# Recurrent layer: ScalarE copies the gate's projection out of its bank, and VectorE multiplies it from memory

## The chip, the cores and the metric

The kernel runs on one core of a Trainium2 chip. A core has five engines with a queue of instructions each: TensorE (PE in the profile, with PEld for its weight loads), VectorE (DVE), ScalarE (ACT), GpSimd (POOL) and SyncE (SP, which issues DMAs here). Each engine works through its queue in order, and semaphores hold an instruction back until what it needs is done. TensorE writes its results into banks of an accumulation memory (PSUM); the other tiles lie in on-chip memory (SBUF). The metric is the device time of one execution in microseconds (us).

## The reference

Four layers run one after the other on x (32 x 64 x 256) with a context of the same shape: a cross-attention of channels (L0), two decoder layers with self-attention, cross-attention and an MLP (L1, L2), and a recurrent layer (L3). Only L3 matters here. Cut to that, it is:

```python
xn  = _ln(x, ln1_w, ln1_b)
sx  = _token_shift(xn, state[:, i1])
xxx = tanh((xn + sx * maa_x) @ maa_w1)          # five mixes of 32 each
xxx = matmul(xxx.reshape(b, l, 5, 1, 32), maa_w2).reshape(b, l, 5, E)
x5  = xn[:, :, None] + sx[:, :, None] * (maa_stack + xxx)
w   = exp(-exp(time_decay + tanh(x5[:, :, 1] @ decay_w1) @ decay_w2))
r, k, v = x5[:, :, 3] @ Wr.T, x5[:, :, 0] @ Wk.T, x5[:, :, 2] @ Wv.T
g   = silu(x5[:, :, 4] @ Wg.T)                  # the gate
# along the sequence, for each head, with a_t = k_t (outer) v_t:
#   out_t = r_t . (u * a_t + s);   s = a_t + w_t * s
att = groupnorm(outs) * gn_w + gn_b
x   = x + att * g @ Wo.T
xn2 = _ln(x, ln2_w, ln2_b);  sx2 = _token_shift(xn2, state[:, i0])
rr  = sigmoid((xn2 + sx2 * ffn_maa_r) @ ffn_Wr.T)
kk  = square(relu((xn2 + sx2 * ffn_maa_k) @ ffn_Wk.T))
return x + rr * (kk @ ffn_Wv.T)
```

## The kernel before

The 2048 tokens are held in four groups; the recurrent layer takes them in eight chunks of 256 tokens (four sequences of 64), numbered n = 0 to 7. A chunk's tiles are [128, 2, 256] in fp32: 128 of the 256 channels on the partitions, the two halves of the channels, and the tokens. In the profile a tile's name ends in `_r` for all chunks alike (`gt_r`, `pg_r`).

The function `recurrent` returns three lists of steps for a chunk. The first holds `norm`, `first_mix`, `maa`, `mix(2, 3)`, `vals`, `mix(0, 1)`, `recept`, `keys`, `mix(4)`, `decay_a`, `decay_b`, `own_term` and `gate`. Four of them use `project`, which multiplies a mix by a weight into a bank: `vals` (bank `pv`), `recept` (`pr`), `keys` (`pk`) and `gate` (`pg`). ScalarE copies `pr` to `rT` (L729); VectorE multiplies `pk` by `rT` into `rk` (L736), which the matmul of `own_term` reads into `pcf` (L742). The mixes are evacuated by VectorE (L689), then GpSimd adds the normed x (L692).

The gate works with a tanh, since silu(p) is half of p * (tanh(p / 2) + 1); the half lies in the weights of the group norm. ScalarE makes the tanh from the bank (L772), and VectorE adds 1 and multiplies by the projection, read from the bank a second time (L773). The result `gt` is needed much later, when `norm_b` multiplies the attention by it (L834).

The second list holds the recurrence: DMAs spread the values over the heads into `vb` (L725), VectorE multiplies them by the keys (L782 in `outer`), ScalarE writes four columns of the state s0 into them (L787), VectorE runs four scans along the tokens (L797) and multiplies by the recept `rT` (L782 again, in `read`), and TensorE sums over the keys into `pa` (L132). This is done for e = 0 and 1. Then come the group norm (L815 to L834) and the output projection `pwo` (L843). The third list is the feed-forward part with `pkk`, `pfr` and `pfv`.

Banks are taken from rings: the tag `mm` has two, `sc` two, `tp` two, `pc` and `pd` one each. `project` takes `mm` for `vals`, `recept`, `keys` and `gate`; the MLP halves of layer L2 (`pln_L2m` for their norm, `pf_L2m` for their hidden layer), which run interleaved with the first chunks, take `mm` too. Whoever takes a bank waits for the last reader of the tile that had it before. Tiles in SBUF are taken from rings in the same way: `gt` has two buffers, `rk` one.

All steps get a due time in units of a chunk's slot, are sorted by it (`timed`, `emit`), and a scheduler that estimates times then sets the order on every engine.

Of the kernel before, what the change touches and what calls it, by code (L numbers as in the profile page):

```python
# [18 lines left out]
ALU = mybir.AluOpType  # L19
# [61 lines left out]
def tile_xattn_stack(ctx: ExitStack, tc: tile.TileContext, a: dict, out: bass.AP):  # L81
    nc = tc.nc
# [519 lines left out]
    def recurrent(n, pool, c3):  # L602

        g, u = n // 2, n % 2
# [11 lines left out]
        def tile_(name, bufs=2, shape=None, p=pool, tag=None):  # L616
            return p.tile(shape or [P, 2, RR], FP, tag=tag or name, name=f"{name}_{t}", bufs=bufs)
# [82 lines left out]
        def project(w, x, name, tag="mm"):  # L700
            ps = both(f"p{name}_{t}", tag)
            for o in range(2):
                project_T(ps[:, o], c3[w], slice(o * P, (o + 1) * P), x)
            return ps
# [63 lines left out]
        def gate():  # L768

            gt = st["gt"] = tile_("gt")  # L770
            ps = project("Wg", st["x5", 4], "g")
            nc.scalar.activation(gt, ps, AF.Tanh, scale=0.5)  # L772
            nc.vector.scalar_tensor_tensor(gt, gt, 1.0, ps, ALU.add, ALU.mult)  # L773

        first = [(0.5, lambda: norm("x", "L3_ln1_w", "L3_ln1_b", t, 1)), (0.0, first_mix), (1.2, maa)]
        first += [(0.85, lambda: mix(2, 3)), (1.7, vals), (0.85, lambda: mix(0, 1)), (1.7, recept), (1.7, keys)]
        first += [(0.85, lambda: mix(4)), (0.5, decay_a), (0.85, decay_b), (0.85, own_term), (1.7, gate)]


# [460 lines left out]
```

## Time and profile before

| | us |
|---|---|
| runs | 1083.98, 1085.02, 1078.87 (median 1083.98) |
| the profiled execution | 1080.68 |
| its span | 1078.9 |
| recurrent layer with the last MLP halves | about 705 to 1079 |
| gates (L772 to L773), first and last start | 749.1 to 1035.3 |

An engine's busy time says how much it works, not what sets the end. For that one reads the chain that ended last, which follows each instruction back to what released it, and the waits: which engine stood still, before which instruction, and what ended it. The timeline of a short window shows the queues side by side. Its columns are the start, the time taken, the engine, the line, the operation, the tiles written and read, the shape and the number of instructions merged in the row; in brackets stands the idle time of the engine before it, and the line that ended that. Rows of several instructions are merged over others in between, so a row's time can hold gaps.

### The profile page before, as it was taken

To read this page: it belongs to the slowest core of one execution; us is meant where nothing else is said; L and a number is where in the kernel's file an instruction comes from. 1 tells how busy PE (TensorE), PEld (TensorE's weight loads), DVE (VectorE), ACT (ScalarE), POOL (GpSimd) and SP (SyncE) were. 2 spreads that over 40 slices of the span, in tenths; PEclk is the share of its full clock that TensorE was granted. 3 is DMA by queue.
4 is the path that set the end of the run, shared out by engine and by line. 5 is a ranking of instruction groups with operands and counts; after the bars stand their busy time and mean duration, and the time that the engine had idled before them with its cause. 6 is when DMAs were issued, how large, how long until landed. Compare 5 with 4: busy or idle time off the path is not lost.

```text
span 1078.9 us, 26319 instructions
## 1 busy us (share of the span) xinstructions
PE 983.6 (91%) x10764; PEld 787.8 (73%) x10764; DVE 806.2 (75%) x1513; ACT 549.2 (51%) x1271; POOL 532.2 (49%) x552
## 2 busy tenths in 40 slices
PE   8998999899989999989989999898989898988966
PEld 4886776667778989877767778787768677765645
DVE  5864688878877654777787887647887987999983
ACT  4743653554456644864454555454436464453334
POOL 4343766767657344756577665442434434153200
PEclk9999998999999999989899999999889999998889
DMA  9300111111100100140111101112122121332400
GB/s 301 105 21 21 23 45 32 38 25 27 26 22 7 40 1 21 46 138 22 41 39 28 26 21 32 31 36 66 41 70 60 50 61 40 95 76 69 98 11 29
DMA packets 45947, 53.39 MB, mean 49 GB/s; under 512 B 16146, under 2 KB 40068, under 8 KB 43780
## 3 DMA queue, kind: packets, MB, share of 16 engines
q1 hardware_dynamic: 40292, 49.60, 17.1%
q10 hardware_dynamic: 5536, 2.12, 0.8%
q8 instruction: 85, 1.39, 0.5%
q14 instruction: 34, 0.28, 0.1%
HBM read 38.83 MB, written 4.21 MB: 40 GB/s over the span
## 4 chain that ended last, share of the span: by engine, by line
PE 43%; DVE 32%; ACT 8%; POOL 8%; issue 4%; DMA 3%; SPq 0%; ACTq 0%; POOLq 0%; DVEq 0%
DVE vb_r L797 6%; PE pf_L1m L187 4%; PE pf_L2m L187 3%; DVE vb_r L782 3%; PE pfo_L1m L187 3%; POOL s_L2c L463 2%; DVE x L198 2%; POOL s_L1c L463 2%; PE pr L312 2%; PE pfo_L2m L187 2%; PE pwo_r L843 1%; PE px_r L132 1%; PE pq_L1c L187 1%; DVE s_L1c L458 1%; POOL s_L1s L463 1%
## 5 line engine op out<-in xcount | busy, mean ns | idle before, releaser
L692 POOL TENSOR_TENSOR x_r<-x_r,xn_r 128x512 f32<-128x512 f32 x40 | 63.6, 1604 | 113.7 <-DVE x_r L689 111.8
L797 DVE TENSOR_TENSOR_SCAN vb_r<-wsh,vb_r 128x512 f32<-128x512 f32 x64 | 77.6, 1276 | 5.6 <-ACT wsh L696 4.1
L463 POOL TENSOR_TENSOR s_L1s<-s_L1s,n 128x512 f32<-128x512 f32 x32 | 43.0, 1356 | 39.9 <-DVE s_L1s L458 39.2
L187 PE MATMUL pf_L2m<-lnT_L2m,w_L 128*128 128x256 f32 x384 | 57.8, 303 | 1.7 <-ACT vbd L430 0.7
L187 PEld LDWEIGHTS pf_L2m<-lnT_L2m,w_L 128*128 128x128 f32 x384 | 51.8, 202 | 7.6 <-issue 2.5
L187 PE MATMUL pfo_L2m<-w_L,hT_L2m 128*128 128x256 f32 x384 | 55.2, 291 | 1.5 <-DVE hT_L2m L581 1.5
L463 POOL TENSOR_TENSOR s_L2s<-s_L2s,n 128x512 f32<-128x512 f32 x32 | 43.0, 1360 | 26.9 <-DVE s_L2s L458 26.3
L187 PE MATMUL pfo_L1m<-w_L,hT_L1m 128*128 128x256 f32 x384 | 54.5, 288 | 1.6 <-POOL hT_L1m L580 0.8
L187 PE MATMUL pf_L1m<-lnT_L1m,w_L 128*128 128x256 f32 x384 | 51.9, 288 | 3.9 <-ACT hf_L1m L577 1.2
L463 POOL TENSOR_TENSOR s_L2c<-s_L2c,n_L2c 128x512 f32<-128x512 f32 x32 | 41.6, 1320 | 27.6 <-DVE s_L2c L458 26.7
L463 POOL TENSOR_TENSOR s_L1c<-s_L1c,n_L1c 128x512 f32<-128x512 f32 x32 | 41.3, 1309 | 25.8 <-DVE s_L1c L458 24.8
L187 PEld LDWEIGHTS pf_L1m<-lnT_L1m,w_L 128*128 128x128 f32 x384 | 47.5, 191 | 7.2 <-ACT hf_L1m L577 2.1
L187 PEld LDWEIGHTS pfo_L2m<-w_L,hT_L2m 128*128 128x128 f32 x384 | 48.7, 190 | 5.2 <-issue 2.7
L187 PEld LDWEIGHTS pfo_L1m<-w_L,hT_L1m 128*128 128x128 f32 x384 | 49.3, 191 | 3.4 <-POOL hT_L1m L580 1.0
L580 POOL TENSOR_SCALAR hT_L1m<-hf_L1m 128x512 fp32r<-128x512 f32 x32 | 21.8, 682 | 55.4 <-ACT hf_L1m L577 53.5
L577 ACT ACTIVATE hf_L1m<-pf_L1m,b_L 128x256 f32<-128x256 f32 x64 | 26.6, 471 | 42.3 <-PE pf_L1m L187 39.9
L581 DVE TENSOR_TENSOR hT_L1m<-hf_L1m,hT_L1m 128x512 fp32r<-128x512 f32 x32 | 25.3, 791 | 30.1 <-POOL hT_L1m L580 30.1
L581 DVE TENSOR_TENSOR hT_L2m<-hf_L2m,hT_L2m 128x512 fp32r<-128x512 f32 x32 | 24.7, 772 | 26.7 <-POOL hT_L2m L580 26.6
L580 POOL TENSOR_SCALAR hT_L2m<-hf_L2m 128x512 fp32r<-128x512 f32 x32 | 22.2, 694 | 40.1 <-ACT hf_L2m L577 39.8
L577 ACT ACTIVATE hf_L2m<-pf_L2m,b_L 128x256 f32<-128x256 f32 x64 | 26.6, 472 | 28.5 <-PE pf_L2m L187 23.0
L782 DVE TENSOR_TENSOR vb_r<-vb_r,ksh 128x2048 f32<-128x2048 f32 x16 | 38.3, 2409 | 2.7 <-DMA vb_r<-vd_r 2.7
L282 ACT ACTIVATE att<-pe,nmx 128x256 f32<-128x256 f32 x64 | 29.5, 476 | 19.3 <-DVE nmx L280 17.2
(388 smaller groups left out, 3062.1 us busy)
## 6 DMA issues: line engine op xcount, KB each, us to landing
vb_r<-vd_r SPq DMA_DIRECT2D x16, 1024.0 KB
raw_w_L<-in_L_w_dram SPq DMA_DIRECT2D x4, 1024.0 KB
y<-in_y_dram SPq DMA_DIRECT2D x8, 256.0 KB
x<-in_x_dram SPq DMA_DIRECT2D x8, 256.0 KB
ctxT_L1c<-in_yT_dram SPq DMA_DIRECT2D x4, 512.0 KB
kbd<-kT_L1s SPq DMA_DIRECT2D x64, 32.0 KB
kbd<-kT_L1c SPq DMA_DIRECT2D x64, 32.0 KB
kbd<-kT_L2s SPq DMA_DIRECT2D x64, 32.0 KB
```

What stands on the lines that cost most here:

```text
L132: return lambda: nc.tensor.matmul(ps, sta, mov, start=start, stop=stop)
L187: nc.tensor.matmul(ps, sta[x], mov[y], start=(at == 0), stop=(at == n - 1))
L198: nc.vector.tensor_tensor(xs, xs, ps, ALU.add)
L282: nc.scalar.activation(att[:, 2 * h + c, :], pe[:, c, :], AF.Exp, bias=nmx[:, h, c : c + 1], accum_out=rs[:, h, c : c + 1],)
L312: nc.tensor.matmul(pr[:, m, h, :], att[:, 2 * h + c, m * P : (m + 1) * P], xvT[:, c, h, :], start=(c == 0), stop=(c == 1),)
L463: nc.gpsimd.tensor_tensor(s[:, r], s[:, r], n(j).unsqueeze(1).broadcast_to([P, 8, S]), ALU.add)
L577: nc.scalar.activation(raw[:, i], ps[:, i], AF.Gelu_apprx_tanh, bias=w()["b1"][:, 2 * f2 + i : 2 * f2 + i + 1])
L580: nc.gpsimd.tensor_scalar(h[:, 0], raw, 1.0, 0.0, ALU.mult, ALU.add)
L581: nc.vector.tensor_tensor(h[:, 1], raw, h[:, 0], ALU.subtract)
L692: nc.gpsimd.tensor_tensor(d, d, st["x"], ALU.add)
L782: nc.vector.tensor_tensor(v, v, x.unsqueeze(1).broadcast_to([P, 4, 2 * RR]), ALU.mult)
L797: nc.vector.tensor_tensor_scan(v[:, d], flat(st["wsh"]), v[:, d], 0.0, ALU.mult, ALU.add)
```

## The change

In `gate`, ScalarE also copies the projection from its bank to SBUF, in the buffer of the tag `rk`, and VectorE reads the copy in place of the bank:

```diff
             gt = st["gt"] = tile_("gt")
             ps = project("Wg", st["x5", 4], "g")
             nc.scalar.activation(gt, ps, AF.Tanh, scale=0.5)
-            nc.vector.scalar_tensor_tensor(gt, gt, 1.0, ps, ALU.add, ALU.mult)
+
+            g_ = tile_("g", 1, tag="rk")
+            nc.scalar.copy(g_, ps)
+            nc.vector.scalar_tensor_tensor(gt, gt, 1.0, g_, ALU.add, ALU.mult)
```

Lines below it are three higher afterwards: the copy is L775, the multiply L776, the products by keys and recept L785, the scan L800. Nothing else is edited, but the scheduler sets the order anew. In the built program the recept projections of chunks 1 to 4 wait for a semaphore of VectorE before the change and of ScalarE after it. The order of the instructions stays the same except in the recurrent part, where a few steps move: on ScalarE and TensorE around the decay of chunk 2 (the table load and a half of the Exp of L765 and the small copies of L790 ahead of the eviction of the feed-forward norm), on TensorE `pa` of chunk 4 ahead of the mix of x5_1 of chunk 5, and in the tail ScalarE's square of chunk 7 behind the norm of chunk 6's second half.

## The prediction

> **What bounds the kernel now.** I read the page first: busy shares, then the chain that ended last.
>
> ```profile
> PE 983.6 (91%) x10764; PEld 787.8 (73%) x10764; DVE 806.2 (75%) x1513; ACT 549.2 (51%) x1271; POOL 532.2 (49%) x552
> PE 43%; DVE 32%; ACT 8%; POOL 8%; issue 4%; DMA 3%; SPq 0%; ACTq 0%; POOLq 0%; DVEq 0%
> ```
>
> No engine sets the end alone: the chain goes from TensorE (PE) to VectorE (DVE) and back. The eight gates lie between 749 and 1035 us, so what stands before 740 us stays as it is. The view of the multiply's line says who waits for it, the waits of PE between 740 and 860 us add one entry:
>
> ```profile
> L773 DVE SCALAR_TENSOR_TENSOR gt_r<-gt_r,pg_r x8: 655/674/680, 755.2 to 1035.3; 128x512 f32<-128x512 f32 x8
>   PE pr_r L192: 6.6, 2
> ```
> ```profile
> PE pr_r L192 <- DVE mv_L2m L147: 3.3, 1, 3.3
> ```
>
> So three times PE stands still before the recept projection `pr` of the next chunk: its bank is the one that held the gate's projection `pg`, and VectorE reads `pg` late because long work stands ahead in its queue. (The third wait names `mv_L2m`, the small row just behind the gate's multiply; PE starts 0.15 us after that multiply.) The timeline shows the three places, which I call gates 0, 1 and 2:
>
> ```profile
> 749.11 0.60 ACT L772 ACTIVATE gt_r<-pg_r 128x512 f32<-128x512 f32 x1 [0.66 <-PE pg_r L192]
> 751.69 1.07 PE L132 MATMUL pa_r<-vb_r,sel 128*32 128x256 f32 x16 [0.96 <-DVE vb_r L782]
> 755.21 0.66 DVE L773 SCALAR_TENSOR_TENSOR gt_r<-gt_r,pg_r 128x512 f32<-128x512 f32 x1
> 756.02 3.75 PE L192 MATMUL pr_r<-x_r,Wr 128*128 128x256 f32 x8 [3.26 <-DVE mv_L2m L147]
> ...
> 797.44 0.59 ACT L772 ACTIVATE gt_r<-pg_r 128x512 f32<-128x512 f32 x1
> 799.37 0.68 DVE L773 SCALAR_TENSOR_TENSOR gt_r<-gt_r,pg_r 128x512 f32<-128x512 f32 x1
> 799.96 2.29 DVE L782 TENSOR_TENSOR vb_r<-vb_r,rT_r 128x2048 f32<-128x2048 f32 x1
> 800.19 3.75 PE L192 MATMUL pr_r<-x_r,Wr 128*128 128x256 f32 x8 [3.21 <-DVE gt_r L773]
> ...
> 840.47 0.59 ACT L772 ACTIVATE gt_r<-pg_r 128x512 f32<-128x512 f32 x1
> 845.67 2.29 DVE L782 TENSOR_TENSOR vb_r<-vb_r,rT_r 128x2048 f32<-128x2048 f32 x1
> 845.90 2.57 PE L192 MATMUL pr_r<-x_r,Wr 128*128 128x256 f32 x8 [3.39 <-DVE gt_r L773]
> ```
>
> Stages of the stretch show what the pause does to PE's clock (columns: us, busy PE, PEld, DVE, ACT, POOL with counts, granted clock, DMA share, GB/s):
>
> ```profile
> 755.00:765.00 10.00, 8.98 (x27) 6.99 (x28) 10.00 (x20) 1.20 (x4) 5.14 (x6) 0.50 0.00 1
> 765.00:799.00 34.00, 29.43 (x215) 23.52 (x213) 28.28 (x30) 19.07 (x38) 12.00 (x9) 1.00 0.29 71
> 799.00:806.00 7.00, 5.81 (x25) 3.38 (x26) 6.33 (x12) 0.59 (x1) 1.80 (x2) 0.52 0.00 0
> ```
>
> After gates 0 and 1 the clock is half: the eight `pr` matmuls take 3.75 us, against 1.89 where the clock is full. But DVE is busy 10.00 of 10.00 and 6.33 of 7.00 us there, so what PE gains may end at DVE.
>
> **The change, part by part.** It adds eight ScalarE (ACT) copies, one per chunk. The nearest row is the same copy from a bank:
>
> ```profile
> L712 ACT COPY vT_r<-pv_r x8: 580/584/602, 721.4 to 1002.6; 128x512 f32<-128x512 f32 x8
> ```
>
> Eight times 0.58 is 4.7 us of ACT, in an engine that is 51% busy. The multiply now has both inputs in SBUF. The nearest rows with two such inputs of this size are L885 (median 690 ns against 674 for L773), so DVE neither gains nor loses: 8 times 0.016 is 0.1 us, taken as nothing. The multiply now waits for the copy, with the product by rT and the next mixes behind it in DVE's queue; DVE comes to it after the copy has ended at every gate, by 0.75 us at the tightest (gate 1: 798.6 against 799.37), so the wait adds nothing. The `rk` buffer that the copy borrows is free: `pcf`, its last reader, stands before `pg` in PE's queue, and the next `rk` product stands behind the gate's multiply in DVE's own queue. In the changed program's order `pr` waits for ACT and no longer for DVE, so the change does what it says. No DMA and no queue of SP or POOL is added or passed.
>
> *Gate 0.* The bank comes free at 749.71 + 0.58 = 750.3, PE at 752.76 (end of `pa`). So `pr` starts 3.26 us earlier, and if the clock holds it is done at 754.65 instead of 759.77. Next is the mix of x5_4, whose banks come free at DVE's L689, 756.8 either way, then the hidden layer `pf`, which waits for DVE's L179 (ends 758.17): `pf` starts at 758.3 instead of 761.7, still cold. What is late after that is `pa`, which waits for DVE's product by rT, 764.93 + 2.28 = 767.21; it ran at 770.30. So `pa` gains 3.05 us, and with it the 1 MB transfer that it releases and the product by keys that waited for that (778.72): **-3.05**.
>
> *Gate 1.* ACT ends the copy at 798.03 + 0.58 = 798.6, `pr` starts at 798.75 instead of 800.19. The next `pa` needs DVE until 802.25, and `pwo` needs DVE's second L834 (ends 804.42). `pwo` ran at 805.74; it can run at 804.5: **-1.25**.
>
> *Gate 2.* The copy ends at 841.65, so `pr` starts at 842.5 and ends at 844.4. But `pa` needs the product by rT, 845.67 + 2.29 = 847.96, and the `pf` behind it needs L179 (ends 850.91). `pf` ran at 851.75 and can run at 851.4: **-0.35**. Most of this wait is hidden behind DVE anyway. The copy puts the Ln/Exp pair and the lnT copy behind it 0.58 us later; DVE takes them 2.8 us later, which covers it.
>
> *Gates 3 to 7.* No `pr` waits for DVE there. The copies at 885.1, 967.8, 1004.4 and 1027.7 fall into idle time of ACT (0.98 to 7.6 us), cost nothing, and would cost 0.58 each if ACT were late. At gate 4 (938.73) the copy stands before the evictions L625 and L632 that free the banks of the next mix, and the new order puts `pa` (DVE is done at 940.74) ahead of both mixes. `pwo` then starts at 940.79 + 1.07 + 2.1 = 944.0, against 942.96, and DVE waits for it: **+1.0**.
>
> *Order.* The scheduler also moves steps near chunk 2's decay (820 to 833 us). ACT's table load, one half of the decay's Exp and two small copies now stand ahead of the eviction of xn_fr and sx_fr. sx_fr, done at 825.12, is done at about 827.6, so DVE idles and has three mixes (1.3 us) left in front of the scan that began at 828.01, and one behind it: by the rows 829.3 + 4.57 + 0.44 = 834.3 against 832.58: **+1.7**. In the tail, sq_r7 moves behind xn_fr's two rows (1.08 us); the table loads are the same, and Exp ends at 1057.1 instead of 1056.8: **+0.3**.
>
> Two values are unknown. The multiply may now be held up by POOL: with both inputs in SBUF, L834 ranges from 471 to 1505 ns and L885 to 1293, while rows with an input in a bank stay within 687 (L884) and 484 (L689). Bounds per gate: 0 and 0.6 us; POOL's large adds lie beside only one gate (1014.39), so I take 0 and keep +4.8 as the end. [...] The clock is the other: it is taken as it falls in the rows.
>
> Sum: -3.05 - 1.25 - 0.35 + 1.0 + 1.7 + 0.3 = **-1.65 us**. The profiled execution took 1080.68 us (span 1078.9, 1.8 around it), which gives 1079.0; it lies 3.3 below the median of the three runs, and off that median (1083.98) the sum gives **1082.3**. About 0.5%, 5.4 us, is what a measurement of this kernel can tell from no change; the three runs alone spread over 6.2.
>
> **The rivals.** *Faster: the clock.* Half clock was granted for 10.2 us after gate 0 (754.96 to 765.20), 6.8 after gate 1 and 3.4 after gate 2, 20.5 in all, which is 10.2 us of PE time lost. Without the pauses these may vanish; PE's share of the chain, 43%, makes that -4.4. If the moved steps also cost nothing, the sum is -4.65 - 4.4 = -9.05: 1075. For it: all three cold stretches follow these pauses. Against it: DVE is full there. [...]
>
> *Slower: the pause moves instead of going.* `pr` runs early, and PE then stands before `pa` and `pf`, for 2 us at gate 0 and 3.6 us at gate 2 by the sums above. The half clock then falls on hidden-layer matmuls, which are on the chain: twelve took 2.87 us cold and 1.45 warm. A cold stretch of 3.4 us on the chain costs 1.7 us. It decides from four more such stretches on: with five, -1.65 + 8.5 = +6.85: 1091. For it: the chain's PE pieces after each gate are `pf`. Against it: gate 0's were cold already.
>
> **How the numbers follow.** The forecast as summed 0.50, the clock 0.28, the moved pause 0.22. Of the forecast's 0.50, errors in six terms of 1 us, POOL's hold and the spread of runs put 0.10 below the 0.5% bound and 0.04 above it. So faster 0.28 + 0.10 = 0.38, same 0.36, slower 0.22 + 0.04 = 0.26. The forecast's own range is 1076 to 1088; with the rivals' prices it is 1074 to 1091.
>
> **What would show it.** `pr` of the next chunk should start at the end of `pa` at gate 0, and PE's waits on `gt_r` should be gone. `pa` should come 3 us earlier after gate 0, with the product by keys at 775.7. The scan of chunk 2 should start late behind DVE's mixes, `pwo` at gate 4 behind the mixes. The new copy should take 0.58 us, the multiply 0.69. Cold stretches gone from 755 to 850 would speak for the first rival; new ones on `pf` for the second. Multiplies over 1 us would make POOL the cause. If the stretch before 740 us changed, all of this would be wrong.

## The result and the profile after

The changed kernel takes 1089.51 us (median; 1086.46 to 1090.84) beside 1083.98 of the kernel before: the ratio is 1.006, with an interval of 1.0037 to 1.0083, so it is about 6.5 us slower by the ratio (the two medians lie 5.5 apart). The profiled execution is one of 1089.51 us with a span of 1087.7. Busy time and chain of the page after:

```profile
PE 988.4 (91%) x10764; PEld 789.9 (73%) x10764; DVE 803.2 (74%) x1513; ACT 553.3 (51%) x1279; POOL 532.5 (49%) x552
PE 41%; DVE 33%; POOL 9%; ACT 8%; issue 4%; DMA 2%; SPq 2%; ACTq 0%; DVEq 0%; POOLq 0%
```

PE has the same 10764 matmuls and needs 4.8 us more for them: the matmuls became slower, not more. The view of the multiply's line, and under it that of the new copy, show what the change was to do:

```profile
L776 DVE SCALAR_TENSOR_TENSOR gt_r<-gt_r,g_r x8: 658/676/684, 757.5 to 1044.3; 128x512 f32<-128x512 f32 x8
  PEld pa_r L132: 0.7, 1
...
L775 ACT COPY g_r<-pg_r x8: 574/580/647, 751.8 to 1034.5; 128x512 f32<-128x512 f32 x8
```

The 6.6 us for which `pr` had waited for this line are gone (so is the third wait, the one that named `mv_L2m`), and both prices are as forecast. The timeline of PE (and one line of DVE) shows gate 0 and gate 2:

```profile
753.85 1.07 PE L132 MATMUL pa_r<-vb_r,sel 128*32 128x256 f32 x16 [0.96 <-DVE vb_r L785]
754.85 1.99 PE L192 MATMUL pr_r<-x_r,Wr 128*128 128x256 f32 x8
760.06 3.33 PE L187 MATMUL pf_L2m<-lnT_L2m,w_L 128*128 128x256 f32 x24
769.02 2.93 PE L187 MATMUL pf_L2m<-lnT_L2m,w_L 128*128 128x256 f32 x12 [2.74 <-ACT hf_L2m L577]
...
842.74 1.89 PE L192 MATMUL pr_r<-x_r,Wr 128*128 128x256 f32 x8
845.90 2.28 DVE L785 TENSOR_TENSOR vb_r<-vb_r,rT_r 128x2048 f32<-128x2048 f32 x1
848.24 1.94 PE L132 MATMUL pa_r<-vb_r,sel 128*32 128x256 f32 x16 [3.61 <-DVE vb_r L785]
852.62 4.85 PE L187 MATMUL pf_L2m<-lnT_L2m,w_L 128*128 128x256 f32 x21
```

`pr` stands right behind the work ahead of it and is warm (at full clock; cold stands for half clock below). But `pa` waits for DVE's product by the recept, and the early bank does not bring that forward, so at gate 2 a pause of 3.61 us now lies in front of `pa`, where it was 3.39 in front of `pr`. Behind it the clock is half for 10.2 us, and the 21 hidden-layer matmuls take 4.85 us in place of 2.78, which stands in the timeline of PE before the change:

```profile
848.41 1.94 PE L132 MATMUL pa_r<-vb_r,sel 128*32 128x256 f32 x16
851.75 2.78 PE L187 MATMUL pf_L2m<-lnT_L2m,w_L 128*128 128x256 f32 x21
```

The windows of the same stretches as before, and of gate 2 (columns as before: us, the engines' busy time, granted clock, DMA share, GB/s):

```profile
755.00:765.00 10.00, 6.91 (x39) 5.59 (x40) 10.00 (x15) 2.92 (x6) 6.26 (x7) 1.00 0.00 1
799.00:806.00 7.00, 5.53 (x37) 3.54 (x36) 7.00 (x11) 2.40 (x5) 0.00 (x0) 1.00 0.00 0
...
847.00:857.50 10.50, 9.26 (x43) 6.93 (x44) 7.32 (x13) 2.07 (x3) 4.00 (x3) 0.51 0.41 100
```

The cold stretches of before are gone from the first two windows (one of 3.4 us now begins at 768.7, on the twelve hidden-layer matmuls of 2.93 us above), and a longer one has come at gate 2. Further on the timeline shows two more, at gate 4 and in the tail:

```profile
944.80 1.07 PE L132 MATMUL pa_r<-vb_r,sel 128*32 128x256 f32 x16 [2.18 <-DVE vb_r L785]
947.50 3.78 PE L846 MATMUL pwo_r<-Wo,at_r 128*128 128x256 f32 x8
953.21 3.56 PE L192 MATMUL pk_r<-x_r,Wk 128*128 128x256 f32 x8
...
1065.30 3.47 PE L846 MATMUL pwo_r<-Wo,at_r 128*128 128x256 f32 x8 [2.38 <-DVE at_r L837]
```

Eight such matmuls take 1.9 to 2.0 us at full clock. In the profile before, `pwo` at gate 4 was cold too (3.54 us) behind a pause of 1.08 us, `pk` was not, and the tail's `pwo` was warm behind a shorter pause:

```profile
939.70 1.13 PE L132 MATMUL px_r<-ta_r,mw2a 32*128 32x256 f32 x4 [1.08 <-ACT xn_r L625]
942.96 3.54 PE L843 MATMUL pwo_r<-Wo,at_r 128*128 128x256 f32 x8
947.48 1.99 PE L192 MATMUL pk_r<-x_r,Wk 128*128 128x256 f32 x8
...
1058.17 1.99 PE L843 MATMUL pwo_r<-Wo,at_r 128*128 128x256 f32 x8 [0.99 <-DVE at_r L834]
```

I followed one instruction through both traces, the large product on VectorE (L782 before, L785 after), and took the difference of its start times, counted from its first one at 736.7 us. The pieces of the profiled execution are: gate 0 -0.35, gate 1 with chunk 2's decay -1.59, gate 2 +2.41, behind it +0.34, gate 3 +1.03, gate 4 +2.88, tail +1.92. Their sum is +6.65. (The two spans differ by 8.8; the other 2.2 us lie ahead of that first product, which starts anywhere from 735.6 to 742.7 us in the sixteen profiles, with the copy and without.)

My theory from this: the pause in front of `pr` was cheap, because `pr` itself took the cold clock, and VectorE was the one that everybody waited for. Moved behind `pr`, the pause stands right in front of work on the chain, and the half clock falls on that. The rivals: the steps that the scheduler moved cost it; or ScalarE's eight copies do.

### The profile page after: what moved, and what is told of

The parts are those of the page before. It is cut to its first block, busy times and chain, and to the rows that moved or that the text cites. A ratio compares the mean times of both kernels' runs of the same rounds, so it can differ in the third digit from the quotient of the medians.

```text
span 1087.7 us, 26328 instructions
## 1 busy us (share of the span) xinstructions
PE 988.4 (91%) x10764; PEld 789.9 (73%) x10764; DVE 803.2 (74%) x1513; ACT 553.3 (51%) x1279; POOL 532.5 (49%) x552
## 4 chain that ended last, share of the span: by engine, by line
PE 41%; DVE 33%; POOL 9%; ACT 8%; issue 4%; DMA 2%; SPq 2%; ACTq 0%; DVEq 0%; POOLq 0%
DVE vb_r L800 7%; DVE vb_r L785 4%; PE pf_L1m L187 4%; PE pf_L2m L187 4%; PE pfo_L1m L187 3%; POOL s_L2c L463 2%; SPq L403 2%; POOL s_L1c L463 2%; PE pr L312 2%; DVE x L198 2%; PE pfo_L2m L187 2%; POOL s_L1s L463 1%; PE pwo_r L846 1%; PE px_r L132 1%; PE pe L132 1%
## 5 line engine op out<-in xcount | busy, mean ns | idle before, releaser
L692 POOL TENSOR_TENSOR x_r<-x_r,xn_r 128x512 f32<-128x512 f32 x40 | 66.8, 1684 | 119.0 <-DVE x_r L689 116.7
L800 DVE TENSOR_TENSOR_SCAN vb_r<-wsh,vb_r 128x512 f32<-128x512 f32 x64 | 78.4, 1286 | 4.7 <-ACT wsh L696 3.2
L187 PE MATMUL pf_L2m<-lnT_L2m,w_L 128*128 128x256 f32 x384 | 60.0, 309 | 5.4 <-ACT hf_L2m L577 3.2
L187 PE MATMUL pf_L1m<-lnT_L1m,w_L 128*128 128x256 f32 x384 | 51.9, 288 | 3.9 <-ACT hf_L1m L577 1.2
L580 POOL TENSOR_SCALAR hT_L1m<-hf_L1m 128x512 fp32r<-128x512 f32 x32 | 21.9, 685 | 55.4 <-ACT hf_L1m L577 53.5
L785 DVE TENSOR_TENSOR vb_r<-vb_r,ksh 128x2048 f32<-128x2048 f32 x16 | 38.3, 2407 | 2.9 <-DMA vb_r<-vd_r 2.9
L580 POOL TENSOR_SCALAR hT_L2m<-hf_L2m 128x512 fp32r<-128x512 f32 x32 | 21.6, 675 | 37.0 <-ACT hf_L2m L577 36.9
```

The lines of the kernel that those rows point to most:

```text
L187: nc.tensor.matmul(ps, sta[x], mov[y], start=(at == 0), stop=(at == n - 1))
L580: nc.gpsimd.tensor_scalar(h[:, 0], raw, 1.0, 0.0, ALU.mult, ALU.add)
L692: nc.gpsimd.tensor_tensor(d, d, st["x"], ALU.add)
L785: nc.vector.tensor_tensor(v, v, x.unsqueeze(1).broadcast_to([P, 4, 2 * RR]), ALU.mult)
L800: nc.vector.tensor_tensor_scan(v[:, d], flat(st["wsh"]), v[:, d], 0.0, ALU.mult, ALU.add)
```

## The experiments

All ratios are to the kernel before, run beside it; 0.001 is 1.08 us. The lines of these kernels lie up to six higher than in the kernel before.

### One gate at a time

Four kernels have the copy at one gate alone; VectorE reads the bank at the others.

```diff
-            g_ = tile_("g", 1, tag="rk")
-            nc.scalar.copy(g_, ps)
+            if n == 0:              # the others: n == 1, n == 2, n == 4
+                g_ = tile_("g", 1, tag="rk")
+                nc.scalar.copy(g_, ps)
+            else:
+                g_ = ps
```

Gate 0, as expected beforehand:

> Only gate 0 has the copy; gates 1 to 7 read the bank as before. The order on every engine is that of before but for the copy itself and neighbours that swap. The prediction's sum asks for -3.05 us. The moved-pause theory: pr early and warm (about 2 us instead of 3.75), but a new wait in front of the second pf, about 2.7 us, because ACT's queue has xn_r standing before hf; so the product by rT that followed at 764.93 may start within +-1 us of where it stood, and the time is within 1 us of before. If ScalarE's extra 0.58 us were on the path, +0.6.

Gate 1, as expected beforehand:

> Only gate 1 has the copy. The scheduler's order moves near chunk 2's decay come with it. Prediction's sum: -1.25 for the gate and +1.7 for the order, +0.45. By the two traces: the gate gives -2.4 and the order takes back 0.8, so -1.6 in all. Theory that the moved steps cost the time: +1.7 or more.

Gate 2, as expected beforehand:

> Only gate 2 has the copy; PE's order is that of before to the instruction. Prediction's sum: -0.35. Moved-pause theory: pr runs before the pause, PE then idles 3.6 us in front of pa, half clock reaches pf (about 10 us instead of 3.4), and all behind it comes 2.4 us later. Theory that moved steps cost it: 0, since none is moved. Theory that the copy itself costs it: +0.6.

Gate 4, as expected beforehand:

> Only gate 4 has the copy; with it pa goes ahead of all of chunk 5's mix matmuls on PE. Prediction's sum: +1.0. Moved-pause theory: the idle time lies before pa, half clock of about 10 us instead of 3.4 covers pwo and pk, and all behind comes 2.9 us later. Copy alone: +0.6.

| copy at | ratio | interval | us |
|---|---|---|---|
| gate 0 | 0.9999 | 0.9978 to 1.0020 | -0.1 |
| gate 1 | 1.0012 | 0.9990 to 1.0035 | +1.3 |
| gate 2 | 1.0036 | 1.0007 to 1.0065 | +3.9 |
| gate 4 | 1.0014 | 0.9993 to 1.0034 | +1.5 |

Gate 0's -3.05 of the forecast and gate 1's -1.6 from the two traces lie outside these intervals. Only gate 2 is clearly apart from no change, and there the order on every engine is that of the kernel before but for the copy, so a moved step can't be the cause. (Its twelve runs lie in two groups, 1078 to 1083 and 1086 to 1091 us; the profiled one, 1083.43, is of the lower group.) The timeline of PE in the kernel with the copy at gate 2 alone shows the same picture as the changed kernel (granted clock 0.50 from 846.4 to 853.2 us):

```profile
839.56 1.89 PE L192 MATMUL pr_r<-x_r,Wr 128*128 128x256 f32 x8
845.22 1.07 PE L132 MATMUL pa_r<-vb_r,sel 128*32 128x256 f32 x16 [3.77 <-DVE vb_r L788]
848.79 4.70 PE L187 MATMUL pf_L2m<-lnT_L2m,w_L 128*128 128x256 f32 x21
```

The other gates are instructive as well. Gate 0 is unchanged in the kernel with the copy at gate 4 alone, and yet its timeline there is not that of the profile before:

```profile
759.39 3.56 PE L192 MATMUL pr_r<-x_r,Wr 128*128 128x256 f32 x8 [3.26 <-DVE mv_L2m L147]
763.94 3.12 PE L187 MATMUL pf_L2m<-lnT_L2m,w_L 128*128 128x256 f32 x24
```

The pause of 3.26 us is there and `pr` is cold, but the hidden layer is warm, and the product by keys behind it comes 2.7 us earlier than in the profile that I forecast from. The same code had a cold stretch of 10.2 us in one execution and of 3.4 us in another (granted clock 0.66 and 0.89 between 753 and 768 us). So I no longer compared two profiles alone, but all that I had.

### The copy without its use, and the pause filled

The first kernel makes the copy at gate 2 and lets VectorE read the bank all the same. The second has the copy at gate 2 in use, and fills the pause: in the built program, TensorE repeats the first pair of matmuls of chunk 3's `pr` (one sum, from start to stop; four matmuls in the profile) three more times. That is useless work, put into PE's queue after the scheduler, so that nothing else moves.

```diff
+            if n == 2:                                     # first kernel
+                g_ = tile_("g", 1, tag="rk")
+                nc.scalar.copy(g_, ps)
+            nc.vector.scalar_tensor_tensor(gt, gt, 1.0, ps, ALU.add, ALU.mult)
...
         tile_xattn_stack(tc, aps, out)                     # second kernel
+    repeat_pair(nc, {"pr_r3": 3})
```

Copy not used, as expected beforehand:

> Gate 2 alone has the copy, but VectorE still reads the bank, so the copy's result is used by nobody and pr of chunk 3 waits for VectorE as before. Every engine's order is that of before plus the one copy. Moved-pause theory: nothing moves, 0 against before (pr again at the end of the pause, half clock behind it about as before). Theory that ScalarE's copy itself costs the time at gate 2: +0.6 or more, up to the +3.9 of the kernel with the copy in use.

Pause filled, as expected beforehand:

> Gate 2 alone has the copy, in use, and TensorE repeats the first two matmuls of pr for chunk 3 three more times (12 hardware matmuls, 2.8 us at full clock, useless work) in the pause of 3.6 us in front of pa. All other orders stay. Moved-pause theory: no stretch of half clock behind gate 2, so -1 to -3 us against before, at least 3 below the kernel without the repeats. If the loss of gate 2 came from anything else than TensorE's clock, the time stays at +3.9, or more by the added work.

The first has a ratio of 0.9987 (0.9967 to 1.0006), the second 0.9993 (0.9971 to 1.0016), where the copy alone had 1.0036. So the copy costs nothing measurable on ScalarE; the early bank costs 3.9 us (0.8 to 7.0 by its interval); and 2.8 us of useless matmuls take that away. The gain of 1 to 3 us that I had expected of them is not shown: -0.7, with no change in the interval. The timeline of PE in the filled kernel:

```profile
843.40 4.48 PE L192 MATMUL pr_r<-x_r,Wr 128*128 128x256 f32 x20
849.07 1.07 PE L132 MATMUL pa_r<-vb_r,sel 128*32 128x256 f32 x16 [1.19 <-DVE vb_r L788]
852.01 2.77 PE L187 MATMUL pf_L2m<-lnT_L2m,w_L 128*128 128x256 f32 x21 [0.26 <-DVE lnT_L2m L179]
```

Twenty matmuls in place of eight, a pause of 1.19 us, and the hidden layer is warm (granted clock 1.00 from 848 to 858 us).

### The whole change without gate 2, and the whole change filled

```diff
-            nc.scalar.copy(g_, ps)                         # first kernel: not at n == 2
+    repeat_pair(nc, {"pr_r1": 2, "pr_r3": 3, "pr_r5": 2})  # second kernel: all copies
```

Without gate 2, as expected beforehand:

> The changed kernel, with the copy left out at gate 2 alone. If the losses add up as the single gates had them (0.0, +1.3, +3.9, +1.5 of about 6.5), the time is 2.6 above before, 3.9 below the changed kernel. If gate 2 is not special and the moved steps or the eight copies cost the time, it stays near +6.

Filled at gates 0, 2 and 4, as expected beforehand:

> The changed kernel with all eight copies and every moved step; TensorE repeats the first pair of matmuls of pr twice at gate 0, three times at gate 2, twice at gate 4 (6.6 us of useless matmuls in the pauses behind pr). Moved-pause theory: mean clock from 0.957 up to 0.967 or so, time at or below before (0 to -4). Theory that moved steps or copies cost the time: +6 as the changed kernel, or more.

Without gate 2 the ratio is 1.0006 (0.9984 to 1.0028). I had expected 2.6 us above before; it is +0.6, so the losses of the single gates do not add up, and leaving out gate 2 takes nearly all of the loss away. (In its profile the tail is 2.05 us late as in the changed kernel, but gate 4 is not late at all.) Seven copies and every moved step are still in it: both rivals fall as the main cause. Its timeline of PE at gate 2 shows how the kernel before hid the cold clock:

```profile
845.20 2.75 PE L192 MATMUL pr_r<-x_r,Wr 128*128 128x256 f32 x8 [3.22 <-DVE gt_r L779]
847.88 1.92 PE L132 MATMUL pa_r<-vb_r,sel 128*32 128x256 f32 x16
851.10 2.78 PE L187 MATMUL pf_L2m<-lnT_L2m,w_L 128*128 128x256 f32 x21
```

`pr` and `pa` take the half clock (granted clock 0.51 from 846.2 to 849.6 us), beside VectorE's work, and the hidden layer comes warm (1.00 from there to 859). Filled at three gates, the whole change has a ratio of 0.9978 (0.9959 to 0.9997): 6.6 us of useless matmuls turn +6.5 us into -2.4. The view of the cores of that kernel has its span and mean granted clock:

```profile
core 0: 1076.5 us, clock 0.972
```

The profile of the changed kernel has 0.958 there.

### The changed kernel again, and the same work where no pause follows

```diff
+    repeat_pair(nc, {"pr_r1": 2, "pr_r3": 3, "pr_r5": 2})  # in the kernel before
```

Changed kernel again, as expected beforehand:

> The changed kernel once more, 12 runs beside the others of this call. +6 us (ratio about 1.006), mean clock 0.956 to 0.958. Moved-pause theory: half clock behind gate 2 for two windows of 3.4 us or more, product by keys behind gate 2 1.4 to 2.4 us late; gates 0, 1 and 4 may look different from the first profile, since they follow where the windows fall.

Kernel before, with the repeats, as expected beforehand:

> The kernel before, with the same useless matmuls in pr that helped the changed kernel (2, 3 and 2 pairs, 6.6 us at full clock). Here pr stands behind the pause, so they can't fill it: moved-pause theory expects them partly on the path, +1 to +5 us. If repeated matmuls helped by themselves (whatever the pause), -2 to -4 as in the changed kernel.

The changed kernel comes out at 1.0073 (1.0047 to 1.0100), 1089.55 us, in six runs. The repeats in the kernel before give 1.0000 (0.9982 to 1.0019): neither the loss that I expected nor a gain. Its timeline of PE at gates 2 and 4 shows why:

```profile
846.19 6.24 PE L192 MATMUL pr_r<-x_r,Wr 128*128 128x256 f32 x20 [3.39 <-DVE gt_r L773]
...
939.52 3.69 PE L192 MATMUL pr_r<-x_r,Wr 128*128 128x256 f32 x16 [0.84 <-issue]
943.15 1.13 PE L132 MATMUL px_r<-ta_r,mw2a 32*128 32x256 f32 x4
946.26 1.99 PE L843 MATMUL pwo_r<-Wo,at_r 128*128 128x256 f32 x8
```

At gate 2 the repeats cost 2.7 us, since `pr` now takes 6.24 us behind the pause. But at gate 4 `pr` stands ahead of the pause in the kernel before too (no `pr` waits for VectorE there), so there the repeats do fill it: `pwo` is warm, and the stage is 1.1 us shorter than in the profile before. My expectation had missed that. So repeats in `pr` help only where a pause follows `pr`; at gate 2 that takes the early bank, at gate 4 it does not. Part of the filled kernel's 2.4 us is therefore no gain of the copy, and whether the kernel before with gate 4 alone filled is as fast was not tried.

### Which pause sets off the loss

```diff
+    repeat_pair(nc, {"pr_r3": 3})                          # first kernel, all copies
+    repeat_pair(nc, {"pr_r1": 2, "pr_r5": 2})              # second kernel, all copies
```

Gate 2 alone filled, as expected beforehand:

> The changed kernel with the three extra pairs at gate 2 alone (2.8 us in the pause of 3.6). If the pause at gate 2 with what it sets off later carries the loss: 5 to 6 us below the changed kernel, that is +0 to +1 against before, no long half clock behind gate 2 and none of three windows behind gate 4. If the pauses at gates 0 and 4 carry their share: about +3.

Gates 0 and 4 filled, as expected beforehand:

> The changed kernel with the two extra pairs at gate 0 and the two at gate 4, and none at gate 2. If gate 2 carries the loss, 10.2 us of half clock stay behind it and the time stays 2 to 5 above before. If the gates 0 and 4 carry it, 0 to -2.

The ratios are 1.0018 (0.9995 to 1.0041) and 0.9991 (0.9975 to 1.0008). I had expected the second to stay 2 to 5 us above before; it did not. Its trace has the loss at gate 2 in full (+2.46, and +1.0 at gate 3). What it saves comes later, at gate 4 and in the tail, as its timeline of PE shows:

```profile
938.91 3.69 PE L192 MATMUL pr_r<-x_r,Wr 128*128 128x256 f32 x16 [0.84 <-issue]
943.06 1.07 PE L132 MATMUL pa_r<-vb_r,sel 128*32 128x256 f32 x16 [0.45 <-DVE vb_r L785]
945.13 1.99 PE L846 MATMUL pwo_r<-Wo,at_r 128*128 128x256 f32 x8
948.11 1.99 PE L192 MATMUL pk_r<-x_r,Wk 128*128 128x256 f32 x8
...
1057.79 1.99 PE L846 MATMUL pwo_r<-Wo,at_r 128*128 128x256 f32 x8 [2.38 <-DVE at_r L837]
```

The pause at gate 4 is 0.45 us and not 2.18, and `pwo` and `pk` are warm; the tail's pause is the same 2.38, and its `pwo` is warm too. But the tail was not filled here, and no half clock fell on its `pwo` all the same (1.99 us, against 3.47 in the changed kernel). So the loss of the changed kernel lies in two parts, from gate 2 to gate 3 and at gate 4 with the tail. Filling gate 2 alone takes most of it away, filling gates 0 and 4 all of it (though with a gain at gate 4 that the kernel before could have too), and filling all three makes the kernel faster than before.

### The last pause

```diff
+    repeat_pair(nc, {"pr_r1": 2, "pr_r3": 3, "pr_r5": 2, "pg_r7": 7})  # all copies
+    repeat_pair(nc, {"pg_r7": 7})                                      # in the kernel before
```

All copies, as expected beforehand:

> The filled changed kernel, with seven more pairs (6.6 us) behind the last gate's projection pg of chunk 7, where TensorE waits 8.6 us for ScalarE's square. If half clock of up to 10.2 us behind that wait lies on the chain, another -2 to -4 us, about 1077. If that stretch is hidden, the same as the filled kernel, 1080.

Kernel before, as expected beforehand:

> The kernel before with only those seven pairs behind pg of chunk 7. -2 to -4 us if the half clock there lies on the chain, 0 if it is hidden. Tells whether the early bank of the change is needed for the gain of the run above.

With all copies the ratio is 0.9978 (0.9958 to 0.9998), the same as without the seven pairs; in the kernel before it is 1.0019 (0.9997 to 1.0042). So the half clock behind the last gate is hidden, and no gain from filling that pause is seen. The two kernels with all copies and filled pauses are the versions that beat both kernels, by 2.4 us against the kernel before.

### All profiles together

The table has the delay of VectorE's large product against the profile of before, stage by stage, in every profile of a kernel without and with the copy at that gate, and with copy and filled pause.

| stage (us in the profile before) | without the copy | with it | with it, filled |
|---|---|---|---|
| gate 0 (752.9 to 778.7) | 0, -2.7, 0.2, -2.7, -2.6, 0.5, -2.7 | -0.4, -2.3, -2.3, -2.4, -2.4 | -1.0, -1.0, -0.9 |
| gate 1 and decay (800.0 to 834.7) | 0, -1.0, -2.6, -0.3, -0.4, -2.6, -0.3 | -1.6, -0.9, -0.8, -0.9, -0.9, -0.9, 1.4, 0.4 | |
| gate 2 (845.7 to 866.1) | 0, 0.1, 0.9, 0.1, 0.0, 0.1, 0.0 | 2.4, 1.4, 2.3, 2.5 | 0.0, 0.4, 0.4, 0.4 |
| gate 4 (938.5 to 951.6) | 0, 1.6, 2.9, 2.9, 1.3, -1.5, 2.9 | 2.9, 2.9, 0.0, 2.9, 1.4 | -1.5, -1.5, -1.5 |

Gate 2 alone is clear-cut: 0 to 0.9 without the copy, 1.4 to 2.5 with it, 0 to 0.4 filled. (The kernel before with the repeats is left out.) At gates 0, 1 and 4 one and the same code differs by up to 4.4 us between executions. The stage at gate 3 (894.8 to 913.9) is 1.0 late in all four profiles with an unfilled copy at gate 2, and -0.1 to 0.6 in all others. With the 0.3 between the two, the changed kernel has lost 2.4 + 0.3 + 1.0 = 3.7 us up to there against the profile before. The kernel with that copy alone has 2.8 in its profile, one of its faster runs, and 3.9 by its ratio.

At gate 4 the half clock alone tells the stage, copy or no copy: where 3.4 us of it follow the stage is 0.0, where 6.8 follow 1.3 to 1.6, where 10.2 follow 2.9, where none follows -1.5.

## Why the prediction was wrong

The mechanism that decided is the second rival, "the pause moves instead of going", which had 0.22 and gave 1091. The forecast, 1082.3, left that price out of its sum: the step that failed is "the clock is the other: it is taken as it falls in the rows". I took the half clock as a fixed property of each gate, and at gate 2 it goes with the pause that the change moves (granted clock 0.51 from 847 to 857.5 us behind the pause, 1.00 from 848 to 858 in the kernel with the pause filled): the term of gate 2, -0.35, came out at +2.4, and at +3.7 up to gate 3. The rival was right in this and not in everything: it saw the half clock fall on the hidden layer, as at gate 2, while at gate 4 it fell on `pwo` and `pk` and in the tail on `pwo`; that its price of five stretches, 6.85 us, meets the 6.5 to 7.9 measured is luck.

**Gate 0, -3.05, was -0.35.** `pr` starts where I put it, and the hidden layer 3.8 us earlier, counted from the first large product. Two things were missed. The profile I read had a draw of 10.2 us of half clock there, and in four of seven profiles without the copy the stage is 2.6 to 2.7 us shorter than in that one. The mean of the seven is -1.4, of the five with the copy -1.9: a gain of 0.5, and none by the medians (-2.6 and -2.3). And the step "what is late after that is `pa`, which waits for DVE's product by rT" skipped ScalarE: its queue holds the normed x of chunk 2 (L155), which waits for VectorE behind four scans, ahead of the hidden layer's eviction; `pf` waits 2.74 us for that bank. I have not tried an order without it. And in every profile with the copy the product by rT starts 0.7 to 0.8 us later than in those without: in the changed kernel the four scans ahead of it took 6.81 us in place of 6.02, beside GpSimd's adds, which start 0.35 us later there, and beside a step of GpSimd (L580) that came only after the scans before. What lengthened the scans is not shown.

**Gate 2, -0.35, was +2.4, and 3.7 with what follows.** I had the new start of `pr`, DVE's end at 847.96 and so the pause of 3.6 us in the text, and then took `pf` as warm. That the pause costs this much is shown by the kernels with the copy alone, with the copy unused and with the pause filled.

**Gate 1 and the order at the decay, -1.25 + 1.7 = +0.45, hold in the sum, by luck.** The order took +0.8 in each profile with that copy, half of the forecast: sx_fr came 1.8 us later, counted from the product by keys ahead of it, and not 2.5. The means of the table are -1.0 without and -0.5 with the copy, +0.5 in all, so the gate itself gained 0.3 and not 1.25.

**Gate 4, +1.0, was +2.9 by the draw, and 0.0 at equal clock.** The changed kernel has +2.9 in both profiles; but three profiles without the copy have 2.9 too, and one with it, where the half clock lasts 3.4 us as in the profile before, has 0.0. With the same length of half clock the stage is the same with the copy and without, within 0.3 us, so the copy and the moved `pa` cost nothing there by themselves. Filled, the stage is 1.5 shorter than before, as it is in one profile without a copy at gate 4 where no half clock followed.

**The tail, +0.3, was +1.9.** The moved square put a pause of 2.38 us in front of `pwo`, where it was 0.99. In three of the seven profiles with that order `pwo` was cold (3.47 us in place of 1.99 in the changed kernel), and the tail was 1.9 to 2.05 longer; in the other four it was warm, and the tail 0.4 shorter than before. So here a moved step does carry a part of the loss, where the half clock falls on `pwo` behind its pause.

**Right:** the early start of `pr`, the vanished waits, the copy's 580 ns hidden on ScalarE (the unused copy cost nothing), the multiply's 676 ns. The hold-up by GpSimd did not come: no multiply took over 684 ns.

The pieces can also be set against more than one profile before: against the mean of the three kernels that use no copy and repeat nothing ahead of the last gate (the kernel before, the unused copy, the kernel before with the seven pairs), the two profiles of the changed kernel are +0.3 at gate 0, -1.0 at gate 1 with the decay, +3.5 from gate 2 to gate 3, +1.7 at gate 4 and +2.1 in the tail, 6.6 in all. The experiments show the 3.5 as the price of the moved pause; for the last two the runs show what they are, a longer half clock, but not that the changed kernel must always draw it.

The mean clock agrees. A mean clock c over a span S costs (1 - c) S of PE's time. Before it is 0.9626 on average over the runs, 40 us; in the changed kernel 0.9564 and 0.9543 in its two sets, 47 and 50 us. That is 7 to 9 us more, and the time grew by 6.5 to 7.9. But it does not tell the time by itself: in the filled kernel it is 0.9712, 31 us, which is 9 less than before for a gain of 2.4, and with the copy at gate 0 alone it is 0.9665, 36 us, for no gain at all. What counts is how much of the half clock lies on the chain.

What remains open: why one and the same step is followed by 3.4, 6.8 or 10.2 us of half clock or by none, whether the longer pause that the change leaves at gate 4 (2.18 us for 1.08) makes the half clock likelier, and whether the changed kernel draws the 10.2 us at gate 4 and the cold `pwo` in the tail each time or only did so in its two profiles.

## What to carry to other kernels

Before a stall is taken away, ask which work follows it: in these traces a stall's cold clock was paid by the next 3.4 to 10.2 us of matmuls, and it cost nothing while those stood beside a busier engine. A bank that comes free early helps little if the next step still waits for the engine that sets the pace; then the pause moves to that wait, here in front of the critical work. And the clock of one profile is a draw (at gate 0 the same code had 10.2 us of half clock in one execution and 3.4 in another): read the same stage in several executions before a cold stretch is put into a sum.

## What the runs showed of the hardware

In the profiles before and after, the half clock from 745 us on comes in stretches of 3.41, 6.83 or 10.24 us (the one in which each profile ends is left out):

| profile | start of the half clock, us (its length) |
|---|---|
| before | 754.96 (10.24), 799.33 (6.83), 847.12 (3.41), 898.32 (3.41), 942.69 (3.41), 973.41 (3.41), 993.89 (6.83), 1014.37 (3.41), 1031.44 (10.24) |
| after | 768.68 (3.41), 789.16 (3.41), 847.19 (10.24), 898.39 (6.83), 946.18 (10.24), 980.31 (3.41), 1000.79 (6.83), 1021.27 (3.41), 1038.34 (10.24), 1065.64 (3.41) |

Ten pauses of PE at gates 0, 1, 2 and 4 and in front of the tail's `pwo`, with the half clock that came in them or within 3 us of their end:

| profile, place | pause, us | half clock, us |
|---|---|---|
| before, gate 0, ahead of `pr` | 3.26 | 10.2 |
| before, gate 1, ahead of `pr` | 3.21 | 6.8 |
| before, gate 2, ahead of `pr` | 3.39 | 3.4 |
| before, gate 4, ahead of `px` | 1.08 | 3.4 |
| before, tail, ahead of `pwo` | 0.99 | none |
| after, gate 0, ahead of `px` | 2.17 | none |
| after, gate 0, ahead of the second `pf` | 2.74 | 3.4 |
| after, gate 2, ahead of `pa` | 3.61 | 10.2 |
| after, gate 4, ahead of `pa` | 2.18 | 10.2 |
| after, tail, ahead of `pwo` | 2.38 | 3.4 |

So in these two profiles the length of the pause alone does not tell the half clock that follows: 2.18 us had 10.2, 2.17 had none.

Both profiles of the changed kernel have the same sequence from gate 2 on: half clock at 847.2, 898.4, 946.2, 980.3, 1000.8 us in the one, and 3.0 to 3.1 us later each time in the other. The cold stretch at gate 2 is not needed for what comes behind gate 4, though: the same sequence from there on (10.2 us, and 34.1 us later 3.4) also stands in the kernel with the copy at gate 4 alone (943.5 and 977.7 us) and in the kernel before with the seven pairs (944.1 and 978.2).

At gate 4 VectorE's product by the recept ahead of `pa` ends at 940.74 us in the profile before, and 3.4 us of half clock begin 1.95 us later; in the profile after it ends at 944.75, and 10.2 us begin 1.43 us later. In the tail `pwo` starts at 1058.17 us before and is warm; after the change it starts at 1065.30, and 3.4 us of half clock begin 0.34 us later. What decides how much half clock a step meets in one execution is not shown, and no run here moves it on purpose.
